# First operands of a gated feed-forward and of causal attention made in the stages in front, zeros in pieces, and sigmoid attention inside a ternary feed-forward

## The chip, the cores and the metric

The kernel runs on one core of a Trainium2 chip. The metric is the device time in microseconds (us) of one execution; less is better. Times of the kernel before are the median of three runs, and the profile is of one more execution.

## The reference

The state x has 2048 tokens of 256 numbers (32 sequences of 64). A second input of the same shape, the context c, is only read. Eight stages follow one another; each adds to x a function of its layer norm:

```
A  x += attention over the 256 columns of each 64-row block, c as keys and values, 8 heads
B  x += down(silu(gate(n)) * up(n)),          n = layernorm(x), 704 hidden
C  x += quantised attention of all 2048 tokens to all of c, 16 heads
D  h = layernorm(x);  h += causal attention(layernorm(h)*w + b) + bo, 16 heads of 128
   x += h + mixture of 4 experts on layernorm(h)
E  x += w_ct(relu(banded attention over the 256 columns of each block) * c)
F  x += ternary feed-forward: quantised rows and weights, 1024 hidden, silu(l0) * l1
G  x += sum over n of c * sigmoid(q^T c / sqrt(64)),  q = layernorm(x)
H  x += mixture of 8 experts (top 2) and a shared expert on layernorm(x)
```

In G each block of 64 rows of the state is its own matrix problem: scores are products of the block's q and c over its 64 rows, the sigmoid is taken of each score times 0.125, and the result is a product of c with these values. D begins with two norms in a row, as the attention norms once more what it is given.

## The kernel before

The state lies in SBUF for the whole run as 16 tiles `xs[i]` of 128 tokens by 256 (`x` in the trace), the context as `cs[i]`. Groups of four tiles (g = 0 to 3) share statistics and the transposed operand `xnT` or `hnT` (128 x 2 x 512). `ln_stats` (L74 to L88) takes a mean and a variance for each tile on DVE, adds epsilon on DVE (L85), and takes the power -1/2 on POOL (L87); `ln_apply` (L91) subtracts and scales on DVE; `transpose_to` (L97) makes two PE transposes, and ACT copies the result out of PSUM.

The stages run in the order of the letters, by the loop at the end of the program: before stage k runs, `weights(k + 1)` allocates the next stage's weights on the other side of SBUF (left and right in turn) and issues their loads on SP's queue. As sides alternate, the loads of stage k + 1 wait for the memory of stage k - 1. H's weights, 5.4 MB, are therefore loaded while G runs.

Outside F a scheduler orders the instructions of each engine from the program's dependences; every engine then works through its own list in order, and a waiting instruction holds those behind it. F is inside `tc.manual_schedule()`: its lists are in the order in which the program issues the instructions.

A (`run_A`) works in slots, step t of a loop of 16 x 8 + 53 steps, and finishes its tiles in order. B (`run_B`) norms a group, makes gate and up products in six chunks, `silu` on ACT (L486), the product on DVE, and four down products. Beside it runs a generator, `keys_and_values`, for stage C: keys, values and their maxima from the context tile by tile (`next(other)`); it begins with one memset of `vz` (L554), 128 x 16384 bf16, the values with zeros around them, and it is stepped once ahead of B's first norm.

C (`run_C`) is a loop over n, 16 tiles times 16 heads, and four steps more: scores on PE (L759), a move with a running maximum on DVE (L789), the exponential on ACT (L813), a cast on POOL (L823), a DMA transpose, and `product` (L772) four steps later. After the last head of a tile come `output`'s steps: a copy, the transposed reciprocal sums `rsT` (L730), two products, and the add to x on POOL (L752).

D begins (`run_D_attention`, `inputs`) with two norms of a group (`hs`, then `hn`), transposes and a scaled copy into `hnT` (L889), four value products (`vp`, L914, with the weights `Dwv`), and projections (L926) with rotations on DVE (`rtq`, L928), ACT and POOL. The bias `bo` is added to `hs` on POOL.

F treats a tile in steps with a lag each, so that step t holds parts of six tiles. For tile i: deviations and a power `s` on POOL; `xk`, two gained copies, their absolute maximum `am`, and the factors `sca` and `dqa` in `scales` (L1272 to L1277); rounding on ACT; transposes `xqT`; products `l` (L1314); `sl` by silu on ACT; `h` on DVE (L1329); squares on ACT; `rr` and `xr` on POOL (L1350, L1344); maximum and rounding `hq` on DVE (L1355, L1358); transposes `hqT`; the product `op`; the sum into x on DVE (L1380). The list of these parts with their lags is the manual order:

```python
for t in range(NT + 6):
    for part, lag in ((summed, 5), (first_transposes, 1), ..., (deviations, -1)):
        if 0 <= t - lag < NT:
            part(t - lag)
```

G (`run_G`) does for each tile: q on DVE, transposes of c and a DVE copy `cT`, eight score products, two sigmoids on ACT, eight products `gop`, and a sum into x on DVE (L1428). H (`run_H`) makes the constant `owner` on POOL (a memset and six selects, L1460 to L1464), norms a group, computes gate logits `hgp`, and runs 14 chunks of gate and up products (`pgate`, `pup`, L1523).

Of the kernel before, what the change touches and what calls it, by code (L numbers as in the profile page):

```python
# [31 lines left out]
def tile_net(ctx: ExitStack, tc: tile.TileContext, a: dict, out: bass.AP):  # L32
# [37 lines left out]


# [331 lines left out]
    def run_A(w, side):  # L403
        with ExitStack() as es:
# [6 lines left out]
            masks = []  # L411
# [18 lines left out]
            def start(t):  # L430
                if t in (16, 18):
                    next(parts)
                if t == 20:
                    for r in range(2):
                        masks.append(cp.tile([P, 1], F32, name=f"gmask{r}"))
                        V.tensor_tensor(masks[r], k["mask"][r], w["gamma"], ALU.mult)

# [16 lines left out]
    def load_B(wp):  # L454
# [8 lines left out]
        w["down_s"] = bcast_row(wp, a["L0_ffn_down_s"], D, "sdown")  # L463
        return w

    def run_B(w, side):
        with tc.tile_pool(name="Bw", bufs=2, side=side) as pool, tc.tile_pool(
# [3 lines left out]
            next(other, None)  # L471
            for g in range(NG):
                ids = range(4 * g, 4 * g + 4)
                xnT = norm_T(pool, psum, ids)
# [30 lines left out]
    def norm_T(pool, psum, ids, src=None, wb=None, keep=None):  # L505
# [3 lines left out]
        xnT = pool.tile([P, 2, 512], F32, name="xnT")  # L509
        for j, i in enumerate(ids):  # L510
# [5 lines left out]
            dst = xnT[:, :, j * P : (j + 1) * P]  # L516
            if wb is None:
                S.copy(dst, tp)
            else:
                for c in range(2):  # L520
                    S.activation(
                        dst[:, c, :], tp[:, c, :], AF.Identity, bias=wb[1][:, c : c + 1], scale=wb[0][:, c : c + 1]
# [21 lines left out]
    def keys_and_values(w):  # L544
# [9 lines left out]
        G.memset(vz, 0.0)  # L554
        w["spread"] = spread = qkp.tile([H, 4, 2, 64], F32, name="spread")
        with tc.tile_pool(name="C1v", bufs=1, side=side) as vp, tc.tile_pool(
# [5 lines left out]
            for i in range(NT):  # L562
# [30 lines left out]
                V.tensor_copy(kT[:, :, i * P : (i + 1) * P], tb)  # L593
                yield
# [49 lines left out]
    def run_C(w, side):  # L644
# [5 lines left out]
        with ExitStack() as es:  # L650
# [17 lines left out]
            with tc.tile_pool(name="C2w", bufs=1, side=side) as pool, tc.tile_pool(  # L668
# [113 lines left out]
                qs = out_ = iter(())  # L782
# [16 lines left out]
                for n in range(N + LAG):  # L799
# [34 lines left out]
                    if h in (0, 2, 3, 4, 5, 7, 8, 10, 11, 12):  # L834
                        next(qs, None)
                for _ in out_:
                    pass


    def load_D(wp):  # L840
# [22 lines left out]
    def run_D_attention(w, side, hs):  # L863
# [4 lines left out]
        with ExitStack() as es:  # L868
# [4 lines left out]
            hnT = [tpool.tile([P, 2, 512], F32, name=f"hnT{g}") for g in range(NG)]  # L873
# [3 lines left out]
            def inputs(g):  # L877
                ids = range(4 * g, 4 * g + 4)
# [767 lines left out]
```

## Time and profile before

| | |
|---|---|
| median of three runs | 2878.74 us (2876.58 to 2881.87) |
| profiled execution | 2879.53 us |
| its span, from first to last instruction | 2877.8 us |
| mean granted TensorE clock | 0.962 of full speed |

| stage | us from the span's start | PE busy | DVE | ACT | POOL | clock |
|---|---|---|---|---|---|---|
| A | 0 to 301.5 | 242.3 | 221.6 | 159.2 | 164.4 | 0.98 |
| B, keys of C | to 521.9 | 188.3 | 120.3 | 41.9 | 82.5 | 0.92 |
| C | to 1219.0 | 541.0 | 663.6 | 613.6 | 561.7 | 0.98 |
| D attention | to 1845 | 606.8 | 340.4 | 334.2 | 343.3 | 0.98 |
| D experts | to 2034 | 160.6 | 96.9 | 73.3 | 33.1 | 0.85 |
| E | to 2346.5 | 271.6 | 209.0 | 152.0 | 235.4 | 0.99 |
| F | to 2495.3 | 93.0 | 135.1 | 86.2 | 61.1 | 0.82 |
| G | to 2555.6 | 49.0 | 29.0 | 18.7 | 13.6 | 1.00 |
| H | to 2877.8 | 315.7 | 98.6 | 52.5 | 11.5 | 0.99 |

Busy times are us in the stretch. PE is TensorE's matmuls (PEld its weight loads), DVE VectorE, ACT ScalarE, POOL GpSimd, SP the engine that issues the DMAs. In a line of the timeline the first number is the start in us from the span's start, the second the time to the end of that instruction or, with xN, of N like it in a row; then engine, line of the program, operation, output, inputs and shapes; in brackets how long the engine had been idle and what released it. L numbers are lines of the kernel before.

### The profile page before, as it was taken

How to read it: one execution, taken by the hardware profiler on the slowest of the kernel's cores; microseconds unless marked ns; L12 is line 12 of the kernel's file. 1: busy time of each engine (PE TensorE's matmuls, PEld its weight loads, DVE VectorE, ACT ScalarE, POOL GpSimd, SP SyncE). 2: the span in 40 equal slices, each digit the busy share in tenths (PEclk: the TensorE clock that was granted, in tenths of full speed). 3: DMA queues.
4: the chain of work that ended last, by engine and by line, in shares of the span. 5: the costliest groups of instructions: out<-in, count | busy, mean ns of one | idle time of the engine just before them, and what ended most of it. 6: DMA issues, size and time to landing. Idle time of an engine off the chain costs nothing.

```text
span 2877.8 us, 44432 instructions
## 1 busy us (share of the span) xinstructions
PE 2468.2 (86%) x16072; PEld 1449.1 (50%) x16072; DVE 1914.5 (67%) x3989; ACT 1531.7 (53%) x2145; POOL 1506.4 (52%) x1681
## 2 busy tenths in 40 slices
PE   4989798777778777689999999789888976789999
PEld 2545344344444444346666666556555533445555
DVE  7877554699999999775455455663577669833332
ACT  1657221599999999655555555353345556521110
POOL 4655433588888888665555555311587754400000
PEclk9999899999999999889999999888999988999999
DMA  6553000499999999910000000001443300200000
GB/s 166 128 116 70 23 1 1 106 202 203 202 207 201 204 201 199 186 59 8 15 15 15 8 1 1 30 30 24 103 93 89 92 1 1 76 1 8 8 8 8
DMA packets 610599, 223.70 MB, mean 78 GB/s; under 512 B 547366, under 2 KB 600524, under 8 KB 605772
## 3 DMA queue, kind: packets, MB, share of 16 engines
q1 hardware_dynamic: 607308, 220.07, 35.0%
q8 instruction: 127, 2.08, 0.3%
q10 hardware_dynamic: 3072, 0.79, 0.2%
q14 instruction: 92, 0.75, 0.1%
HBM read 66.91 MB, written 18.87 MB: 30 GB/s over the span
## 4 chain that ended last, share of the span: by engine, by line
PE 50%; DVE 22%; issue 9%; POOL 5%; ACT 2%; DMA 1%; ACTq 0%; DVEq 0%; POOLq 0%; SPq 0%
DVE e L789 11%; PE yp L985 4%; PE ppq L926 3%; PE ppk L926 3%; PE hout L1502 3%; PE vp L914 3%; PE pgate L1523 3%; PE pup L1523 3%; PE sp L944 2%; PE ep L1072 2%; PE op L970 2%; PE hmp L1065 2%; PE sc L759 1%; PE op L495 1%; POOL e L286 1%
## 5 line engine op out<-in xcount | busy, mean ns | idle before, releaser
L813 ACT ACTIVATE ei<-e,nb,sq 128x2048 int16<-128x2048 f32 x256 | 535.4, 2092 | 43.4 <-DVE nb L810 39.7
L823 POOL CAST eb<-ei 128x2048 bf16<-128x2048 int16 x256 | 482.5, 1895 | 116.1 <-ACT ei L813 102.0
L759 PE MATMUL sc<-kT,qz 128*128 128x512 bf16 x1024 | 298.1, 382 | 142.0 <-DVE e L789 139.9
L246 DVE TENSOR_REDUCE negm<-s 128x2 f32<-128x512 f32 (+1 forms) x512 | 300.9, 611 | 130.6 <-PE s L242 127.4
L789 DVE TENSOR_SCALAR_CACHE_REDUCE e<-sc,mx 128x1024 f32<-128x1024 f32 x256 | 326.1, 1274 | 0.8 <-DVE nb L810 0.7
L789 DVE TENSOR_SCALAR_CACHE_REDUCE e<-sc 128x1024 f32<-128x1024 f32 x256 | 312.4, 1220 | 10.5 <-PE sc L759 10.5
L278 ACT ACTIVATE e<-s 128x1024 f32<-128x1024 f32 (+1 forms) x256 | 233.2, 915 | 152.8 <-PE s L274 117.3
L242 PE MATMUL s<-stk,stq 96*128 96x256 bf16 (+1 forms) x1024 | 192.2, 271 | 41.2 <-DMA d3k<-t3k 24.8
L759 PEld LDWEIGHTS <-qz 128*128 128x128 bf16 x1024 | 94.9, 97 | 261.2 <-issue 202.6
L934 POOL TENSOR_TENSOR rwq<-rwq,sin 128x512 f32<-128x512 f32 x64 | 81.1, 1268 | 240.1 <-ACT rwq L931 203.7
L274 PE MATMUL s<-stq,stk 128*128 128x256 bf16 (+1 forms) x1024 | 180.6, 262 | 10.8 <-DMA stq<-nm 5.4
L772 PEld LDWEIGHTS <-vz 128*64 128x64 bf16 x4096 | 123.2, 110 | 114.0 <-issue 113.9
L946 DVE TENSOR_REDUCE mx<-sp 128x4 f32<-128x512 f32 x64 | 44.3, 692 | 192.7 <-PE sp L944 192.7
L772 PE MATMUL av<-eT,vz 128*64 128x128 bf16 x4096 | 164.0, 223 | 7.3 <-DMA eT<-eb 7.2
L87 POOL TENSOR_TENSOR rstd<-ve,mhalf 128x1 f32<-128x1 f32 (+1 forms) x56 | 42.4, 757 | 240.9 <-DVE ve L85 145.9
L931 ACT ACTIVATE rwq<-ppq,dbq 64x512 f32<-64x512 f32 x128 | 87.4, 683 | 148.9 <-DVE rtq L928 148.0
L1533 DVE TENSOR_TENSOR hm<-pup,sl 128x512 f32<-128x512 f32 (+1 forms) x56 | 38.7, 692 | 191.1 <-PE pup L1523 187.4
L242 PEld LDWEIGHTS <-stq 96*128 96x128 bf16 x1024 | 93.6, 101 | 131.9 <-issue 108.6
L296 PE MATMUL o<-e,vmo 128*32 128x256 f32 (+1 forms) x2048 | 151.1, 367 | 7.4 <-POOL e L286 6.0
L1531 ACT ACTIVATE sl<-pgate 128x512 f32<-128x512 f32 (+1 forms) x56 | 33.4, 597 | 219.2 <-PE pgate L1523 219.1
L286 POOL TENSOR_SCALAR_AFFINE_SELECT e<-e 128x256 f32<-128x256 f32 (+1 forms) x256 | 133.2, 547 | 31.0 <-ACT e L278 30.3
L914 PE MATMUL vp<-Dwv,hnT 128*128 128x512 f32 x256 | 123.8, 605 | 4.0 <-ACT hnT L889 4.0
(349 smaller groups left out, 5518.5 us busy)
## 6 DMA issues: line engine op xcount, KB each, us to landing
stk<-d3k SPq DMA_DIRECT2D x96, 192.0 KB
stq<-d3q SPq DMA_DIRECT2D x96, 192.0 KB
d3k<-t3k SPq DMA_DIRECT2D x160, 64.0 KB
d3q<-t3q SPq DMA_DIRECT2D x96, 64.0 KB
eT<-eb SPq DMA_TRANSPOSE x256
fw<-in_L_ffn_w SPq DMA_DIRECT2D x3, 1024.0 KB
x<-in_x SPq DMA_DIRECT2D x16, 128.0 KB
c<-in_ctx SPq DMA_DIRECT2D x16, 128.0 KB
```

Of the source, the lines that this page charges most:

```text
L242: PE.matmul(sc[:, hh, lo:hi], qs[0:96, 2 * hp + hh, qc * P : (qc + 1) * P], ks[0:96, 2 * hp + hh, lo:hi], start=band is None, stop=True, s ...
L246: V.tensor_reduce(negm[:, qc, 2 * hp : 2 * hp + 2], sc[:, :, lo:hi], AX.X, ALU.max, negate=True)
L274: PE.matmul(sc[:, c, lo:hi], ks[:, h, lc * P : (lc + 1) * P], qs[:, h, lo:hi], start=True, stop=True)
L278: S.activation(e[:, :, lo:hi], sc[:, :, lo:hi], AF.Exp, scale=scale)
L759: PE.matmul(sc[:, k0 : k0 + 512], qz[i % 2][:, h, :], kT[:, h // 2, 1024 * part + k0 : 1024 * part + k0 + 512], start=True, stop=True,)
L772: PE.matmul(av[i][r0 : r0 + 64, h // 4, :], vz[:, kt, h // 4, h % 4, :], eT[:, kt, :], start=h == 0 and kt < 2, stop=h == H - 1 and kt >= ...
L789: V.tensor_scalar(e, scs.pop((n, part)), 1.0, mx[:, 0:1] if part else LOWEST, ALU.mult, ALU.max, accum_out=mx[:, part : part + 1],)
L813: S.activation(ei, es_.pop(n), AF.Exp, bias=nb, scale=sq[i][:, h : h + 1], accum_out=sums[i][:, h : h + 1],)
L823: G.tensor_copy(eb, eis.pop(n - 1))
L914: PE.matmul(vp, hnT[g][:, c, j * P : (j + 1) * P], wv[:, c, :], start=c == 0, stop=c == 1)
L926: PE.matmul(pp, wt[:, c, hh * P : (hh + 1) * P], hnT[g][:, c, :], start=c == 0, stop=c == 1)
L1523: PE.matmul(pp[:m], w[nm + "s"][:, c, cols], xnT[:, c, :], start=c == 0, stop=c == 1)
```

## The change

The dictionary `heads` hands work of a stage to the stage in front.

- B's first `xnT0` is made by `norm_parts` in A's last loop steps, from step 146, in A's pools. The keys of C start with B's first chunk instead of ahead of its norm.
- The memset of `vz` is split into one for each tile, issued as the keys are made.
- D's first `hnT0` is made by `inputs_D` in C's last loop steps (n of 256 and up), two of its steps each, in buffers of C. It computes the first norm into temporaries; D itself then computes the first norm again, into `hs`, and adds `bo`. The loads of the experts' weights are issued later in the program.
- G's parts are added to F's list, with lags 5 to 7 and a loop of NT + 8 steps; G itself returns at once. The sigmoid becomes 0.5 + 0.5 tanh(z/2): the half is taken by half row sums of c, from an ACT accumulation. Here q is made on POOL, `cT` copied on ACT, the result scaled on ACT (`gy`), and added to x on POOL. G's PSUM tiles share the tags of F's (`xqT`, `hqT0`, `hqT1`, `op`).
- In `scales` a tensor_scalar with the column `s` becomes a scalar_tensor_tensor with `s` broadcast.

```diff
@@ -68,6 +68,8 @@
+    heads = {}
@@ -408,7 +410,7 @@
             parts = attention_constants(cp, k)
-            masks = []
+            masks, head = [], []
@@ -435,6 +437,11 @@
+                if t == 146 and "B" in heads:
+                    head.append(heads.pop("B")(pool, psum))
+                if head:
+                    next(head[0], None)
@@ -461,6 +468,8 @@
         w["down_s"] = bcast_row(wp, a["L0_ffn_down_s"], D, "sdown")
+        w["xnT0"] = wp.tile([P, 2, 512], F32, name="xnT0")
+        heads["B"] = lambda pool, psum: norm_parts(w["xnT0"], pool, psum, "tp", range(4))
@@ -468,10 +477,14 @@
             other, stats = beside.pop() if beside else (iter(()), iter(()))
-            next(other, None)
+            if "B" in heads:
+                for _ in heads.pop("B")(pool, psum):
+                    pass
             for g in range(NG):
+                if g == 1:
+                    next(other, None)
                 ids = range(4 * g, 4 * g + 4)
-                xnT = norm_T(pool, psum, ids)
+                xnT = norm_T(pool, psum, ids, dst=None if g % 2 else w["xnT0"], bufs=1) if g else w["xnT0"]
@@ -502,24 +515,35 @@
-    def norm_T(pool, psum, ids, src=None, wb=None, keep=None):
+    def norm_parts(dst, pool, psum, tag, ids):
+        mv, rstd = ln_stats(pool, [xs[i] for i in ids], "hd")
+        yield
+        for j, i in enumerate(ids):
+            xn = pool.tile([P, D], F32, name="hdn", bufs=2)
+            ln_apply(xn, xs[i], mv, rstd, j)
+            yield
+            S.copy(dst[:, :, j * P : (j + 1) * P], transpose_to(psum, xn, tag, f"hdT_{i}"))
+        yield
+    def norm_T(pool, psum, ids, src=None, wb=None, keep=None, dst=None, bufs=2):
...
         mv, rstd = ln_stats(pool, [src[i] for i in ids])
-        xnT = pool.tile([P, 2, 512], F32, name="xnT")
+        xnT = pool.tile([P, 2, 512], F32, name="xnT", bufs=bufs) if dst is None else dst
...
@@ -551,7 +575,6 @@
         w["vz"] = vz = qkp.tile([P, NT, 4, 4, 64], BF, name="vz")
-        G.memset(vz, 0.0)
@@ -591,6 +614,7 @@
                 V.tensor_copy(kT[:, :, i * P : (i + 1) * P], tb)
+                G.memset(vz[:, i], 0.0)
@@ -779,7 +803,7 @@
                 scs, mxs, es_, eis, eTs = {}, {}, {}, {}, {}
-                qs = out_ = iter(())
+                qs = out_ = head = iter(())
@@ -833,6 +857,17 @@
                         next(qs, None)
+                    if n == N and "D" in heads:
+                        own = dict(stats=(small, H, "amq"), bn=(small, H, "rsq"), h=(pool, D, "xn"), hn=(pool, D, "qq"))
+                        def tile(nm):
+                            home, width, name = own[nm]
+                            return home.tile([P, width], F32, name=name)
+                        head = heads.pop("D")(tile, psum)
+                    if n >= N:
+                        next(head, None)
+                        next(head, None)
@@ -849,14 +884,63 @@
         w["gate"] = load(wp, [P, 2, 4], a["L1_ffn_w_gate"].rearrange("(c p) e -> p c e", p=P), "dgate")
+        w["hnT0"] = wp.tile([P, 2, 512], F32, name="hnT0")
+        heads["D"] = lambda tile, psum: inputs_D(w, None, w["hnT0"], 0, tile, psum)
...
+    def inputs_D(w, hs, hnT, g, tile, psum):
+        first = [None] * 4
+        for k in range(2):
+            t = tile("stats")
+            mv, ve, rstd = t[:, 0:8].rearrange("p (j c) -> p j c", c=2), t[:, 8:12], t[:, 12:16]
+            for j in range(4):
+                src = xs[4 * g + j]
+                if k == 1:
+                    src = first[j] if hs is not None else tile("h")
+                    if hs is None:
+                        V.tensor_scalar(src, xs[4 * g + j], *factors[j], ALU.subtract, ALU.mult)
+                b6 = tile("bn")[:, 0:6]
+                V.bn_stats(b6, src)
+                V.bn_aggr(mv[:, j, :], b6)
+                if j == 1:
+                    yield
+            V.tensor_scalar(ve, mv[:, :, 1], 1e-5, None, ALU.add)
+            G.tensor_tensor(rstd, ve, mhalf[:, 0:4], ALU.pow)
+            yield
+            if k == 0:
+                factors = [(mv[:, j, 0:1], rstd[:, j : j + 1]) for j in range(4)]
+                if hs is not None:
+                    for j in range(4):
+                        first[j] = hs[4 * g + j]
+                        V.tensor_scalar(first[j], xs[4 * g + j], *factors[j], ALU.subtract, ALU.mult)
+        for j in range(4):
+            if hs is None:
+                first[j] = tile("h")
+                V.tensor_scalar(first[j], xs[4 * g + j], *factors[j], ALU.subtract, ALU.mult)
+            hn = tile("hn")
+            V.tensor_scalar(hn, first[j], mv[:, j, 0:1], rstd[:, j : j + 1], ALU.subtract, ALU.mult)
+            if hs is not None:
+                G.tensor_tensor(first[j], first[j], w["bo"], ALU.add)
+            tp = transpose_to(psum, hn, "tp", f"hnTp_{4 * g + j}")
+            for c in range(2):
+                S.activation(
+                    hnT[:, c, j * P : (j + 1) * P], tp[:, c, :], AF.Identity,
+                    bias=w["ln1_b"][:, c : c + 1], scale=w["ln1_w"][:, c : c + 1],
+                )
+            yield
...
         with tc.tile_pool(name="Dh", bufs=1, side=side) as hpool:
-            w["we1"] = load(hpool, [P, 2, 4, D], a["L1_ffn_we1"].rearrange("(c p) e i -> p c e i", p=P), "we1")
-            w["be1"] = load(hpool, [P, 4, 2], a["L1_ffn_be1"].rearrange("p (e c) -> p e c", c=2), "be1")
-            w["be2"] = load(hpool, [4, D], a["L1_ffn_be2"].rearrange("o e d -> (o e) d"), "be2")
...
+            def experts():
+                w["we1"] = load(hpool, [P, 2, 4, D], a["L1_ffn_we1"].rearrange("(c p) e i -> p c e i", p=P), "we1")
+                w["be1"] = load(hpool, [P, 4, 2], a["L1_ffn_be1"].rearrange("p (e c) -> p e c", c=2), "be1")
+                w["be2"] = load(hpool, [4, D], a["L1_ffn_be2"].rearrange("o e d -> (o e) d"), "be2")
+            w["experts"] = experts
@@ -870,26 +954,16 @@
             psum = es.enter_context(tc.tile_pool(name="Dp", bufs=1, space=PSUM))
-            hnT = [tpool.tile([P, 2, 512], F32, name=f"hnT{g}") for g in range(NG)]
+            hnT = [w["hnT0"]] + [tpool.tile([P, 2, 512], F32, name=f"hnT{g}") for g in range(1, NG)]
...
             def inputs(g):
-                ids = range(4 * g, 4 * g + 4)
-                mv, rstd = ln_stats(pool, [xs[i] for i in ids])
-                for j, i in enumerate(ids):
-                    ln_apply(hs[i], xs[i], mv, rstd, j)
-                mv, rstd = ln_stats(pool, [hs[i] for i in ids])
-                for j, i in enumerate(ids):
-                    hn = pool.tile([P, D], F32, name="hn")
-                    ln_apply(hn, hs[i], mv, rstd, j)
-                    G.tensor_tensor(hs[i], hs[i], w["bo"], ALU.add)
-                    tp = transpose_to(psum, hn, "tp", f"hnTp_{i}")
-                    for c in range(2):
-                        S.activation(
-                            hnT[g][:, c, j * P : (j + 1) * P], tp[:, c, :], AF.Identity,
-                            bias=w["ln1_b"][:, c : c + 1], scale=w["ln1_w"][:, c : c + 1],
-                        )
+                for _ in inputs_D(w, hs, hnT[g], g, tile, psum):
+                    pass
+            def tile(nm):
+                return pool.tile([P, D if nm[0] == "h" else 16], F32, name=f"in_{nm}")
@@ -986,7 +1060,15 @@
             weights_of(0)
-            inputs(0)
+            if "D" in heads:
+                heads.pop("D")
+                inputs(0)
+            else:
+                mv, rstd = ln_stats(pool, [xs[j] for j in range(4)])
+                for j in range(4):
+                    ln_apply(hs[j], xs[j], mv, rstd, j)
+                    G.tensor_tensor(hs[j], hs[j], w["bo"], ALU.add)
+            w["experts"]()
@@ -1272,7 +1356,7 @@
                 V.reciprocal(sc, am)
-                V.tensor_scalar(sc, sc, s, 127.0, ALU.mult, ALU.mult)
+                V.scalar_tensor_tensor(sc, sc, 127.0, s.to_broadcast([P, n]), ALU.mult, ALU.mult)
@@ -1380,14 +1464,73 @@
+            def g_norm(i):
+                d = st[i]
+                mv, rstd = ln_stats(pool, [xs[i]], "g")
+                V.tensor_scalar(mv[:, :, 0], mv[:, :, 0], -1.0, None, ALU.mult)
+                d["q"] = pool.tile([P, D], F32, name="gq")
+                G.tensor_scalar(d["q"], xs[i], mv[:, 0, 0:1], rstd, ALU.add, ALU.mult)
+            def g_context(i):
+                d = st[i]
+                d["ctp"] = psum.tile([P, 2, 2, P], F32, tag="xqT", name="gcT")
+                for c in range(2):
+                    PE.transpose(d["ctp"][:, 0, c, :], cs[i][:, c * P : (c + 1) * P], ident)
+            def g_context_copy(i):
+                d = st[i]
+                d["cT"] = pool.tile([P, 2, P], F32, name="cT")
+                S.copy(d["cT"], d["ctp"][:, 0])
+                junk = tpool.tile([P, D], F32, name="gjunk")
+                d["half"] = pool.tile([P, 1], F32, name="half", bufs=3)
+                S.activation(junk, cs[i], AF.Identity, scale=0.5, accum_out=d["half"])
+            def g_scores(i):
+                d = st[i]
+                d["sp"] = []
+                for b in range(2):
+                    rows = slice(64 * b, 64 * b + 64)
+                    sp = psum.tile([P, 4, P], F32, tag=f"hqT{b}", name=f"gsp{b}").rearrange("p (n a) t -> p n (a t)", n=2)
+                    for n in range(2):
+                        PE.matmul(sp[:, n, :], d["q"][rows, n * P : (n + 1) * P], cs[i][rows, :], start=True, stop=True)
+                    d["sp"].append(sp)
+            def g_tanh(i):
+                d = st[i]
+                d["sg"] = []
+                for b in range(2):
+                    sg = pool.tile([P, 2, D], F32, name=f"gsg{b}")
+                    S.activation(sg, d["sp"][b], AF.Tanh, scale=0.0625)
+                    d["sg"].append(sg)
+            def g_product(i):
+                d = st[i]
+                d["gop"] = psum.tile([P, D], F32, tag="op", name="gop")
+                for b in range(2):
+                    rows = slice(64 * b, 64 * b + 64)
+                    for n in range(2):
+                        PE.matmul(
+                            d["gop"][rows, :], d["cT"][:, n, rows], d["sg"][b][:, n, :], start=n == 0, stop=n == 1
+                        )
+            def g_sum(i):
+                d = st[i]
+                y = pool.tile([P, D], F32, name="gy")
+                S.activation(y, d["gop"], AF.Identity, scale=0.5, bias=d["half"])
+                G.tensor_tensor(xs[i], xs[i], y, ALU.add)
+            parts = [
+                (summed, 5), (first_transposes, 1), (first_copy, 1), (second_transposes, 4), (second_copy, 4),
+                (hidden, 2), (g_product, 7), (g_sum, 7), (hidden_products, 1), (gates, 1), (second_norm, 3),
+                (squares, 2), (gained, 2), (g_context, 6), (g_context_copy, 6), (first_sizes, 0), (first_rounding, 0),
+                (second_rounding, 3), (g_scores, 6), (g_tanh, 6), (output, 4), (deviations, -1), (g_norm, 5),
+            ]
             deviations(0)
-            for t in range(NT + 6):
-                for part, lag in (
-                    (summed, 5), (first_transposes, 1), (first_copy, 1), (second_transposes, 4), (second_copy, 4),
-                    (hidden, 2), (hidden_products, 1), (gates, 1), (second_norm, 3), (squares, 2), (gained, 2),
-                    (first_sizes, 0), (first_rounding, 0), (second_rounding, 3), (output, 4), (deviations, -1),
-                ):
-                    if 0 <= t - lag < NT:
+            for t in range(NT + 8):
+                for part, lag in parts:
+                    if 0 <= t - lag < NT and (with_g or not part.__name__.startswith("g_")):
@@ -1395,6 +1538,8 @@
     def run_G(w, side):
+        if "FG" in STAGES:
+            return
```

More of the change, by code (lines that the diff above doesn't have):

```diff
@@ L515, in norm_T @@
             tp = transpose_to(psum, xn, "tp", f"xnT_{i}")
-            dst = xnT[:, :, j * P : (j + 1) * P]
+            part = xnT[:, :, j * P : (j + 1) * P]
             if wb is None:
-                S.copy(dst, tp)
+                S.copy(part, tp)
             else:
@@ L521, in norm_T @@
                     S.activation(
-                        dst[:, c, :], tp[:, c, :], AF.Identity, bias=wb[1][:, c : c + 1], scale=wb[0][:, c : c + 1]
+                        part[:, c, :], tp[:, c, :], AF.Identity, bias=wb[1][:, c : c + 1], scale=wb[0][:, c : c + 1]
                     )
@@ L1238, in run_F @@
     def run_F(w, side):
+        with_g = "FG" in STAGES
         if "ternary" in shared:
```

## Prediction

> **What bounds the kernel now.** One execution was profiled: 2879.53 us, a span of 2877.8 and 1.7 outside it. The busy shares of the whole span (PE 86%) say little, as eight stages with different limits follow one another. So I read the view by stretches first, at the seams that the change touches: stage B's start, ternary F, sigmoid G. After the stretch and its length come PE, PEld, DVE, ACT, POOL (busy us, instructions), granted clock, DMA share, GB/s.
>
> ```profile
> 301.00:311.00 10.00, 3.75 (x4) 1.17 (x4) 9.35 (x15) 1.31 (x3) 9.94 (x2) 0.50 0.38 90
> 321.00:331.00 10.00, 7.47 (x23) 2.94 (x21) 5.23 (x16) 2.20 (x7) 4.82 (x7) 0.65 0.00 0
> 331.00:521.00 190.00, 174.09 (x613) 89.34 (x612) 97.19 (x263) 38.44 (x81) 62.23 (x86) 0.98 0.00 1
> 2346.00:2495.00 149.00, 93.39 (x450) 52.76 (x448) 134.87 (x359) 86.22 (x145) 61.06 (x66) 0.82 0.00 1
> 2495.00:2556.00 61.00, 49.21 (x290) 27.89 (x290) 29.34 (x87) 18.67 (x33) 13.56 (x11) 1.00 0.31 90
> ```
>
> B's first 30 us leave PE nearly empty at half clock, and after that it is 92% busy: B is PE's, but for a late start. F is DVE's (134.87 of 149), with PE 63% and POOL 41% busy. G is PE's (49.21 of 61), with DVE half idle. Then the timeline at the seams.
>
> ```profile
> 301.59 13.75 POOL L554 MEMSET vz<- 128x16384 bf16 x1
> 304.02 11.34 DVE L85 TENSOR_SCALAR ve<-mv 128x4 f32<-128x4 f32 x1
> 332.48 0.70 PE L482 MATMUL gp<-xnT,wgate 128*128 128x512 f32 x1
> ```
>
> A 128x4 operation, 0.16 elsewhere, lasts 11.34: it ends as the memset ends. B's norm is behind it, so the first gate product comes 31 us after B begins.
>
> ```profile
> 1207.86 1.06 PE L772 MATMUL av<-eT,vz 128*64 128x128 bf16 x16 [0.95 <-DMA eT<-eb]
> 1217.65 0.35 SPq L107 DMA_DIRECT2D band<-in_c_band  x1
> 1219.03 0.43 DVE L82 BATCH_NORM_STATS2 bnst<-x 128x6 f32<-128x256 f32 x1 [9.59 <-POOL x L752]
> 1223.38 0.52 SPq L107 DMA_DIRECT2D Dwv<-in_L_ffn_wv  x1
> 1228.18 0.46 ACT L889 ACTIVATE hnT<-hnTp,ln_b,ln_w 128x128 f32<-128x128 f32 x1 [10.10 <-DMA Dwv<-in_L_ffn_wv]
> 1243.58 0.73 DVE L928 SCALAR_TENSOR_TENSOR rtq<-ppq,dbq,cos 128x512 f32<-128x512 f32 x1
> ```
>
> C ends with a serial tail, then D's loads on SP and D's norms on DVE run side by side.
>
> ```profile
> 2357.99 2.46 DVE L1284 SCALAR_TENSOR_TENSOR xk<-x,mv,fg 128x256 f32<-128x256 f32 x2
> 2419.29 2.49 POOL L1344 TENSOR_TENSOR xr<-h,fg 128x512 f32<-128x512 f32 x2
> 2420.82 0.99 DVE L1275 TENSOR_SCALAR sca<-sca,s 128x2 f32<-128x2 f32 x1
> 2495.44 1.27 POOL L1460 MEMSET owner<- 96x1408 bf16 x1 [5.78 <-DVE x L1380]
> 2555.21 0.42 DVE L1428 TENSOR_TENSOR x<-x,gop 128x256 f32<-128x256 f32 x1 [2.95 <-PE gop L1425]
> 2562.15 1.20 PE L1523 MATMUL pgate<-xnT,hwgate 128*128 128x512 f32 x1
> ```
>
> In F the 128x2 `sca` again ends with a POOL operation (2421.8). The last three are H's preparations, that start when F ends, G's last sum, and H's first product, 6.5 us after that sum.
>
> **1. A and B: the first xnT made in A's last steps; the memset in 16 pieces.** PE finishes A's own work near 298, and its gate products can then start at about 300 instead of 332.48. What stands in the way is small: 8 transposes on PE, 4 ACT copies of 0.37, 4 statistics of 0.42 and 4 applies of 0.40 on DVE, about 1.5 us where they displace A's last values. B's PE work stays: the 188 busy us in 301 to 521 hold some 14 of start-up, mostly at half clock, that shrink to about 8, so 182; at the 91.6% of the stretch 331 to 521 it lasts 198.6 us. From 301 that ends at 499.6 instead of 520.9: 21 us. Minus the 1.5 leaves 19.5. C's keys, which ran in B's first 30 us, now share B with it; they are covered by PE's own work, but PE, in order, can stall at the first kTp if POOL's chain is late. That is 3 to 6 us if uncovered. The memset pieces are 13.75/16 = 0.86 each; seven stand ahead of the first POOL work of the keys (6.0 us), which no one waits for at once. Bounds: -26 (no stall, better fill) to -12.
>
> **2. C and D: the first hnT made in C's last steps.** The reverse. DVE, POOL and PE are in order, and on PE the transposes hnTp of tiles 0 and 1 stand ahead of C's last product, tiles 2 and 3 ahead of rsT. They need a second norm: four applies and statistics of about 1.0 each on DVE from 1205.05 (after the last moved value), an add of 0.16, a POOL power behind the last cast, so the first hnTp at 1210.9; two transposes and two ACT writes of 0.81 through one bank bring the last product to 1214.3 (begun at 1207.86 before) and rsT to 1217.5 (1208.85). C ends 8.5 us later. Behind it wait: the `band` load at SP's head and, six loads later, `Dwv`, and x15's add on POOL, for which D's statistics wait. Since hnT was held by `Dwv` anyway (10.10 us of wait), having it early brings nothing itself. What is saved is D's second norm of the first group, 4.4 to 4.9 us of the chain on DVE and POOL that runs from 1219.03 to 1263.9 and releases rtq at 1243.58. Net: +8.5 - 4.7 = +3.8, say **+4**; -1 if the tiles go in without delaying the product, +9 if nothing is saved. The expert loads keep their place in SP's order; nothing.
>
> **3. `scales` by another instruction form.** `sca` lasts 0.99 against 0.23 where POOL is free, in 12 of 16 tiles: 9 us at most. The Trainium skill ("SBUF — State Buffer", Who interferes with whom) speaks against a gain: an exclusive port pair is taken by DVE's two-port forms, tensor_scalar among them, and also by a DVE operation with two SBUF inputs against a GpSimd one that reads SBUF. The new form reads `sc` and a broadcast `s`, two SBUF inputs, and `xr` reads SBUF. The trace agrees: the two-input `xk` above took 2.46 for two, where 0.47 is its shortest, under `xr`. By the first half of the rule alone the sum would be -9; by the whole of it, 0. I take 0.
>
> **4. F with G inside it, lags 5 to 7, sigmoid by tanh.** F's period is 8.84 us (L1380's ends from 2380.03 to 2477.33, 11 tiles, 97.3), with DVE full. Per tile G adds on DVE: statistics 0.42, aggregate 0.18, two small ones 0.30, of which 0.41 was there (G's own statistics already ran in F's gaps): DVE alone gives 9.3. POOL gets x's add (0.73), a power (0.55) and q (about 0.7 by the row of the add): 5.5 per tile, no bound; ACT reaches 8.0 (gy 0.47, cT 0.4, half sum 0.65, tanh 1.17), PE 7.9. But the queues are in order and there is a loop: hq of one step, hqT (1.06), gop of the older tile (1.57, from G's row), gy on ACT (0.47), x's add on POOL (0.73), the power (0.66), xr (2.5), amb's reduction and four small ones and hq (2.8), with hand-offs of about 0.1 to 0.2: 10.5. Part of it runs with the previous step, so I take **10.2** between 9.2 (DVE only) and 11.7 (loop plus held `sca`). Then F and G: 11 full steps from 2380, a drain of 2.3 periods (17.5 against 8.84 now is 2.0, plus two more lags), and for the last tile norm, q, scores, tanh, product, sum of 7.7. End = 2380 + 13.3 x 10.2 + 7.7 = 2523.4, against 2555.6: **-32**. The sigmoid's table load (1.28, once) goes too, within this.
>
> **5. What F and G covered.** H's weights (5.4 MB, 340 GB/s from 2495.5 to about 2513) and its constants start when F's memory comes free, and lay beside G. Now they start at G's end. On POOL the order is: owner memset 1.27, five selects of 1.40, and only then H's first power. That is 8.5 us, power 1.0, one apply 0.5, four transposes with copies at 0.9, gate logits 2.7: the first pgate comes 16.4 after G's last sum instead of 6.5. The weights, first needed then, land at +7.5 (gate) and +13 (up): covered. PE is idle for most of it, so its clock falls (0.50 in the first row above); 2 us more. **+12**, from +7 to +17.
>
> Sum: 2879.5 - 19.5 + 4 + 0 - 32 + 12 = 2844.0; the median stands 0.8 under the profiled execution: **2843** (1.2% faster).
>
> **The rivals.**
> *DVE sets F with G (period 9.2).* For it: DVE is 90% busy and POOL 41%. Against: `xr` is waited for already, and one more POOL operation stands ahead of it. End 2510: 2830. Also if the new form of `sca` isn't held.
> *The loop sets it, longer (11.7).* For: every hand-off crosses an engine, and a shared bank (gcT in xqT's, gsp in hqT's, gop in op's) gives PE one more wait each. End 2543.3: 2863.
> *B's start gains little.* The keys' kTp stalls PE as in the stretch 471 to 481, where PE did 5.4 of 10: then -10 instead of -19.5, 2853.
> *Slower.* The loop in F with G: it becomes serial, each tile passing through POOL twice with PE waiting in its queue. The other parts together are -3.5, so F with G decides when its end is later than 2559: a period of (2559 - 2387.7)/13.3 = 12.9, which is 46% over today's. At 13.5 it is 2887. Against it: no single engine has more than 9.3.
> *The change does nothing in C and D* is within the bounds of 2.
>
> **How the numbers follow.** Forecast 50%, short period 20%, long period 14%, B's start 9%, slower 5%, even 2%. A measurement of this kernel tells 0.2%, some 6 us, from no change: faster 0.93, same 0.02, slower 0.05. The range reaches to the short period with part 1's better end, and to the long one: 2818 to 2864.
>
> **What would show it.** Right: first gp at 300 to 303; last av of C near 1214 and band near 1226; L1464's sums every 10.2 in F with G; owner's memset directly after G's last add, and pgate 16 after it; `sca` still near 1 in most tiles. Wrong: a period of 9 or 12, PE waiting for kTp in B, Dwv no later than now, or pgate waiting for hwgate.

## The result, and the profile after

The changed kernel takes 2842.23 us (median of four runs, 2840.02 to 2843.49) against 2879.16 for the kernel before (now four runs): a ratio of 0.9871, with a 95% interval of 0.9854 to 0.9888. The prediction was 2843. The profiled execution of it took 2840.02 us, its span is 2838.3 (before: 2879.53 and 2877.8).

A sum that comes out right may be right by two errors, so I cut the traces at the same instruction in each kernel. All times in the table are from an instruction's start or end in one profile to another's in the same profile.

| stretch | before | after | change | predicted |
|---|---|---|---|---|
| start to A's last add | 301.5 | 298.4 | -3.1 | |
| A's last add to C's first score | 229.3 | 212.3 | -17.0 | -19.5 with the row above |
| C's first score to its last cast | 673.1 | 674.7 | +1.5 | 0 |
| C's last cast to D's first rtq | 39.6 | 44.0 | +4.4 | +4 |
| D's first rtq to F's first xk (D and E) | 1104.3 | 1106.2 | +1.9 | 0 |
| F's first xk to G's last product | 207.3 | 167.5 | -39.8 | -32 |
| G's last product to H's first pgate | 7.0 | 19.5 | +12.6 | +12 |
| pgate to the end of H's last sum | 312.6 | 312.2 | -0.4 | 0 |

A's part scatters by itself: in the profiles of the twelve kernels of the experiments, whose A is the same or nearly so, its last add ends between 294.5 and 298.9, and that of tile 5, long before any edit, between 165.2 and 170.5 over all fourteen. The experiments were also run later than the changed kernel, together with the kernel before, which then took 2874.55 to 2877.39 us (medians of seven runs) instead of 2879.16. So the totals of two kernels of this study say little under some 5 us; those of all twelve lie 2 to 8 us under what their stretches give, and the experiments are read by stretch.

The view by stretches of the kernel after, with the columns as before (length, then PE, PEld, DVE, ACT, POOL, clock, DMA share, GB/s): B's start, B, F with G, H's start.

```profile
294.00:304.00 10.00, 9.49 (x26) 4.04 (x25) 7.26 (x29) 4.34 (x7) 7.99 (x11) 1.00 0.58 158
304.00:334.00 30.00, 24.22 (x74) 10.33 (x73) 17.02 (x44) 6.19 (x14) 20.12 (x27) 0.89 0.00 1
334.00:500.00 166.00, 149.53 (x538) 78.65 (x537) 83.59 (x227) 31.02 (x67) 56.61 (x78) 0.98 0.00 1
2336.00:2494.00 158.00, 116.79 (x692) 66.01 (x692) 141.45 (x391) 112.58 (x228) 85.21 (x107) 0.90 0.00 1
2504.00:2523.00 19.00, 6.44 (x25) 4.85 (x26) 10.59 (x37) 2.77 (x5) 13.05 (x11) 0.57 0.97 285
```

PE is busy from B's first microsecond, at full clock in the first row (in the 30 us behind it 81% and 0.89). F with G is DVE's, 90% busy, with PE at 74% instead of 63. H's start is now bare: PE does 6.4 us of work in 19, at a clock of 0.57, while the weights come in. The timeline at the seams, B, D, F and H in turn:

```profile
294.94 1.98 PE L495 MATMUL gp<-xnT,wgate 128*128 128x512 f32 x4 [0.51 <-ACT rd L311]
298.47 6.35 POOL L617 MEMSET vz<- 128x1024 bf16 x7
301.68 0.45 DVE L87 TENSOR_SCALAR ve<-mv 128x4 f32<-128x4 f32 x1
...
1195.06 1.06 PE L796 MATMUL av<-eT,vz 128*64 128x128 bf16 x16
1207.86 0.36 SPq L109 DMA_DIRECT2D band<-in_c_band  x1
1213.58 0.52 SPq L109 DMA_DIRECT2D Dwv<-in_L_ffn_wv  x1
1218.15 9.57 PE L988 MATMUL vp<-Dwv,hnT 128*128 128x512 f32 x16 [9.22 <-DMA Dwv<-in_L_ffn_wv]
...
2399.73 2.50 POOL L1428 TENSOR_TENSOR xr<-h,fg 128x512 f32<-128x512 f32 x2
2399.96 1.06 DVE L1359 SCALAR_TENSOR_TENSOR sca<-sca,s 128x2 f32<-128x2 f32 x1
...
2504.72 1.27 POOL L1605 MEMSET owner<- 96x1408 bf16 x1
2513.13 2.00 POOL L89 TENSOR_TENSOR rstd<-ve,mhalf 128x4 f32<-128x4 f32 x2
2522.74 3.76 PE L1668 MATMUL pgate<-xnT,hwgate 128*128 128x512 f32 x4
```

The first gate product even precedes A's last add (by 3.5 us). `ve`, that the memset held for 11.34 us, takes 0.45. From `band` to the first `vp` D still waits for `Dwv`, 9.22 us on PE. `sca` in its new form takes 1.06; the old one took 0.99. And `owner` is made ahead of H's first power.

### The profile page after: what moved, and what is told of

Read it like the earlier page. It is cut to its first block, busy times and chain, and to the rows that moved or that the text cites. A ratio compares the mean times of both kernels' runs of the same rounds, so it can differ in the third digit from the quotient of the medians.

```text
span 2838.3 us, 44529 instructions
## 1 busy us (share of the span) xinstructions
PE 2448.6 (86%) x16072; PEld 1439.3 (51%) x16072; DVE 1901.2 (67%) x3986; ACT 1544.1 (54%) x2208; POOL 1533.8 (54%) x1741
## 3 DMA queue, kind: packets, MB, share of 16 engines
q1 hardware_dynamic: 607308, 220.07, 35.5%
## 4 chain that ended last, share of the span: by engine, by line
PE 48%; DVE 22%; issue 9%; POOL 7%; ACT 2%; DMA 1%; SPq 0%; ACTq 0%; DVEq 0%; POOLq 0%
DVE e L813 11%; PE yp L1059 4%; PE ppq L1000 4%; PE ppk L1000 3%; PE hout L1647 3%; PE vp L988 3%; PE pgate L1668 3%; PE pup L1668 3%; PE sp L1018 2%; PE ep L1154 2%; PE op L1044 2%; POOL e L288 2%; PE hmp L1147 2%; PE sc L783 1%; PE op L508 1%
## 5 line engine op out<-in xcount | busy, mean ns | idle before, releaser
L1678 DVE TENSOR_TENSOR hm<-pup,sl 128x512 f32<-128x512 f32 (+1 forms) x56 | 38.7, 691 | 190.6 <-PE pup L1668 186.9
L89 POOL TENSOR_TENSOR rstd<-ve,mhalf 128x1 f32<-128x1 f32 (+1 forms) x44 | 29.9, 680 | 178.7 <-DVE ve L87 86.2
```

## The experiments

Twelve kernels, each an edit of the changed kernel.

**1. The first norm back in B (e1), and the memset in one piece again (e2).**

```diff
-                if t == 146 and "B" in heads:
+                if t == 1460 and "B" in heads:
```
```diff
+        G.memset(vz, 0.0)
...
-                G.memset(vz[:, i], 0.0)
```

> Against the changed kernel (2842.2): B's first norm is put back into B, the memset stays in pieces and the keys still start with the first chunk. If the early norm itself is what moved B's start, B waits again for statistics, power, applies and four transposes, about 7 to 8 us after A's last add, and the first gate product comes near 306 instead of 294.9: 2850 to 2853. If most of the old 31 us came from the memset ahead of the norm, that is all that is lost; if the two are worth the same, the whole 20 us of part 1 come back: 2862.

> Against the changed kernel: the memset of vz is one piece again (13.75 us), the early norm stays. If the memset matters only because B's norm stood behind it, nothing is lost: 2842 within 3. If it still holds a 128x4 operation on DVE for its whole length, B's products hT stand behind that on DVE, PE's banks fill, and 8 to 10 us come back: 2850 to 2852.

Measured: 2847.06 and 2846.12 us. From A's last add to C's first score they take 223.1 and 219.7 instead of 212.3: the early norm is worth 10.7 us, the pieces 7.4, together 18.1, about the 17.0 that the changed kernel gained in this stretch. That C's keys start with B's first chunk, as they do in all three kernels, wasn't tried alone. The first gate product of e1 comes at 306.7, 11.3 after A's last add (7 to 8 expected). In e2 it comes as early before that add as in the changed kernel, and then:

```profile
297.06 13.75 POOL L578 MEMSET vz<- 128x16384 bf16 x1
300.26 10.57 DVE L87 TENSOR_SCALAR ve<-mv 128x4 f32<-128x4 f32 x1
```
```profile
304.00:314.00 10.00, 0.57 (x3) 0.60 (x4) 9.96 (x17) 0.00 (x0) 6.81 (x1) 0.66 0.00 0
```

The first fence is its timeline, the second its stretch from 304 to 314. A `ve` of a later norm is held until the memset ends at 310.8, the `vall` of C's keys and B's products `hT` stand behind it on DVE, and PE does 0.57 us of work in 10: it waits 9.8 us, to the end of `vall`. The memset stalls B even if B's own first norm is long done.

**2. Without the early hnT (e3), and with its transposes later (e7).** In e3 D makes its own; in e7 the first norm's statistics and half of the second's stay in C's last steps, and the rest comes behind C's output.

```diff
-                    if n == N and "D" in heads:
+                    if n == N + 100 and "D" in heads:
```
```diff
                     if n >= N:
-                        next(head, None)
-                        next(head, None)
+                        next(head, None) if n < N + 3 else None
                 for _ in out_:
                     pass
+                for _ in head:
+                    pass
```

> Against the changed kernel: D makes its first hnT itself, as before. By part 2 of the prediction C's last product and rsT are no longer delayed (8.5 us) and D's start takes its second norm back (4.7): 2838.4, faster by 3.8; C's last product ends near 1189 instead of 1196.1. If the early hnT is a gain, as the change has it, it is slower by 4 to 9: 2846 to 2851.

> Against the changed kernel: the early hnT stays in C's tail, but its transposes stand on PE behind C's last product, rsT and op. By part 2 the delay of C's end goes (8.5 us from the last cast to the last product, as in the run without the early hnT) and the second norm stays saved: from the last cast to rtq 36 us, against 44.0 in the changed kernel and 39.6 in before: 2834. If the delay comes from DVE or POOL rather than PE's order, the last product still ends 10 us after the last cast: 2842.

Measured: 2830.26 and 2831.33 us. C's last product ends 4.95 and 4.89 us after its last cast, as before the change (4.94), against 10.69 with the early hnT in its place: PE's order was the delay. From the last cast to rtq e3 takes 39.6, 4.5 us less than the changed kernel (3.8 expected); the rest of its lead in the profiles lies in A, B and C (3.2) and behind rtq (2.2), where the other kernels differ as much. But e7 takes 40.2, not 36: its delay is gone, and the early operand still brings nothing. Its timeline says why:

```profile
1192.74 0.35 SPq L109 DMA_DIRECT2D band<-in_c_band  x1
1195.10 0.41 DVE L924 TENSOR_SCALAR qq<-xn,amq 128x256 f32<-128x256 f32 x1 [9.28 <-POOL amq L911]
1201.17 0.75 DVE L84 BATCH_NORM_STATS2 bnst<-x 128x6 f32<-128x256 f32 x2 [1.23 <-PE hnTp L99]
1201.22 0.38 SPq L109 DMA_DIRECT2D Dwv<-in_L_ffn_wv  x1
1215.44 1.88 PE L1001 MATMUL ppq<-hnT,Dwq 128*128 128x512 f32 x4
1219.38 0.72 DVE L1003 SCALAR_TENSOR_TENSOR rtq<-ppq,dbq,cos 128x512 f32<-128x512 f32 x1
```

`rtq` doesn't wait for `ppq`, which ends at 1217.32; it follows DVE's other work without a pause. DVE reaches D's own statistics only at 1201.17, 8.4 us behind `band` (1.4 in the changed kernel), since the early applies, each waiting for the transposes of the one before, now stand between C's end and D: what D is spared is done just ahead of it. `Dwv` is issued 8.5 us behind `band` instead of 5.7, after the last of these transposes; why it waits for them wasn't tried, and it isn't what `rtq` waited for.

**3. G after F again (e4).**

```diff
-        with_g = "FG" in STAGES
+        with_g = False
...
-        if "FG" in STAGES:
-            return
```

> Against the changed kernel: G runs after F again, with its sigmoid; everything else stays. F's period goes from 9.35 to 8.8 and G takes its 60 us, H's constants and weights lie beside G: F's start to pgate takes 214.3 as before instead of 187.1, so 27 us come back: 2869. If H's late start has another cause than the lost cover, pgate stays 16 us behind G's last sum and it is 2879.

Measured: 2862.89. F's first xk to pgate takes 214.1 us (before 214.3; changed 187.1): the 27 us are these two parts and nothing else (the total, 2869 expected, is lower by the other stretches). pgate follows G's last product after 8.0.

**4. The old form in scales, and DVE's order.** In e8 the line of `scales` is the old one. In e5 the operations stay and DVE's order changes: the new entries split `first_sizes`, `second_rounding`, `deviations` and `g_norm` behind their reductions.

```diff
-                (first_sizes, 0), (first_rounding, 0),
-                (second_rounding, 3), (g_scores, 6), (g_tanh, 6), (output, 4), (deviations, -1), (g_norm, 5),
+                (first_sizes, 0), (second_size, 3),
+                (deviation_stats, -1), (g_stats, 5), (first_scales, 0), (first_rounding, 0),
+                (second_rounding, 3), (g_scores, 6), (g_tanh, 6), (output, 4), (deviation_power, -1), (g_norm, 5),
```

> Against the changed kernel: scales has its tensor_scalar back, all else stays. By part 3 both forms are held by xr alike: sca near 1.0 in most tiles, and 2842 within 3. If the new form is what freed DVE, it is 8 to 11 us slower: 2850 to 2853.

> Against the changed kernel: DVE's order in F with G. The reduction of xr (of the step before) and the two pairs of statistics, that read one tile each, are put between the maximum am and the factor sca, so that they run while POOL makes xr, and the small operations on two SBUF inputs come after it. If DVE's own list, with sca's 0.83 us of being held, sets the period, as the trace of the changed kernel has it (DVE busy 94%, nothing waited for), sca takes about 0.2 and the period falls from 9.35 to about 8.5: 11 us less, 2831. If the loop through PE, ACT and POOL of the prediction is what binds, the period stays, and sca, 2.4 us later in the step, makes the rounding and PE later: 2842 to 2850.

e8 measured 2837.13 us; F with G takes 168.3 against 167.5, and the group of `sca` between 2370 and 2480 (busy, mean ns, idle) is, in the changed kernel and in e8:

```profile
L1359 DVE SCALAR_TENSOR_TENSOR sca<-sca,s 128x2 f32<-128x2 f32 x11 | 11.5, 1043 | 0.4
```
```profile
L1359 DVE TENSOR_SCALAR sca<-sca,s 128x2 f32<-128x2 f32 x11 | 11.6, 1053 | 0.4
```

The two forms are held alike, as the Trainium skill ("SBUF — State Buffer", Who interferes with whom) has it for a two-port form and for two SBUF inputs. e5 measured 2827.94; its F with G takes 159.5, 8.0 less, at a median period of 8.62 instead of 9.35. DVE's list was the bound. But the holding, which was expected to go, only moved: what came next was held instead. Lines of the changed kernel, then of e5:

```profile
2408.05 0.69 DVE L1370 TENSOR_REDUCE am<-xk 128x2 f32<-128x512 f32 x1
2408.84 0.23 DVE L1356 TENSOR_SCALAR am<-am,s 128x2 f32<-128x2 f32 x1
```
```profile
2406.19 0.69 DVE L1377 TENSOR_REDUCE am<-xk 128x2 f32<-128x512 f32 x1
2406.80 1.21 DVE L1449 TENSOR_REDUCE amb<-xr 128x1 f32<-128x1024 f32 x1
2407.54 2.50 POOL L1438 TENSOR_TENSOR xr<-h,fg 128x512 f32<-128x512 f32 x2
2409.00 1.07 DVE L1363 TENSOR_SCALAR am<-am,s 128x2 f32<-128x2 f32 x1
2410.31 0.16 DVE L1366 SCALAR_TENSOR_TENSOR sca<-sca,s 128x2 f32<-128x2 f32 x1
```

`sca` is at 0.16, and a tensor_scalar on 128x2, 0.23 in the changed kernel, waits for the end of `xr` at 2410.04 (in some steps both are held). The two changes cancel. The 0.7 us that the step lost are mostly pauses: an operation that needs the result of a reduction starts 0.1 us after its end, one that doesn't starts 0.08 before it. From the start of `am`'s reduction to the next operation it is 0.61 instead of 0.79, for `amb`'s 1.13 instead of 1.32, for each of the two aggregates 0.10 instead of 0.22. In the first two full steps of e5, when POOL has no sums of G yet, nothing is held, and the period is 7.75.

**5. H's start.** Three kernels: `owner` issued after the first group's norm (e6); H on the side of SBUF that nobody uses while F with G runs, its loads issued at F (e9); the same with H's working buffers on F's side (e12, the second diff besides the first).

```diff
-        return ("left", "right")[STAGES.index(stage) % 2]
+        return "left" if stage == "H" else ("left", "right")[STAGES.index(stage) % 2]
...
+            if STAGES[k] == "F":
+                ahead[k + 2] = weights(k + 2)
```
```diff
-            pool = es.enter_context(tc.tile_pool(name="Hw", bufs=2, side=side))
+            pool = es.enter_context(tc.tile_pool(name="Hw", bufs=2, side="right"))
```

> Against the changed kernel: the constant owner (a memset and six selects on POOL) is issued after the first group's norm in H instead of ahead of it. By part 5 of the prediction POOL's 8.4 us stand between G's last sum and the first power; without them the first pgate comes about 10 us after G's last sum instead of 18, unless it then waits for hwgate, expected at 7.5: 2834 to 2836. If the weights set it anyway, at most 2 us are won: 2840.

> Against the changed kernel: H's weights and constants get the other side of SBUF, which nobody uses while F with G runs, and are loaded and made during F. If H's late start is the loss of the cover that G gave (part 5 of the prediction, +12.6 as measured from G's last sum to pgate), it comes back: pgate about 7 us after G's last product, as before, or sooner: 2828 to 2832. If the first group's norm, that waits for the last tiles or for memory, is what takes the time, owner's absence only saves POOL's part, about 3 us as in the run with owner later: 2839.

> As the run on the free side, against the changed kernel, but H's working buffers lie on F's side again, so that its statistics can't be put into F's lists; weights, owner and share stay on the free side. In that run F's period was 10.6 to 12.2 instead of 9.35, with DVE waiting at H's statistics of a tile for G's sum of that tile. If these statistics in DVE's queue are the cause, the period is 9.35 again, G's last product is 52 us ahead of before's, and pgate follows it after 13 to 16 us (norm and transposes are no longer hidden, owner and the weights are): 2835 to 2838. If the loads or POOL's constants beside F slow it, the period stays above 10: 2848 or more.

e6 measured 2834.32: pgate 16.8 after G's last product instead of 19.5. The scheduler still put the memset and two selects ahead of the first power, which comes 4.2 us after G's last sum instead of 8.5; and the first two applies of the norm, under the other selects, take 2.82 us instead of 0.74. So only part of the 8.4 us went. e9 measured 2845.67, no gain: pgate comes 7.5 after G's last product, as expected of the lost cover, but F with G takes 185.5 instead of 167.5. With the memory free, H's statistics were put into DVE's list in F:

```profile
2397.37 0.43 DVE L84 BATCH_NORM_STATS2 bnst<-x 128x6 f32<-128x256 f32 x1 [1.30 <-POOL x L1522]
```

They need G's sum of the tile, which is late in the step, and DVE, the bound, stands still for it (9.0 us in nine steps) besides the time that they take themselves. In e12 they stay out: 2834.28, a period of 9.34 again in most steps (one of 10.57), F with G 171.5, pgate 13.5 after G's last product. So the loads and the constants beside F cost no more than 4 us; the rest of the 18 is H's early norm, the statistics and what follows them.

**6. Together.** e10 is without the early hnT and has a further order in F: on DVE the gained copies and `sca` ahead of `h`, on PE `l` last in a step. e11 has H on the free side besides.

```diff
+                (g_product, 7), (g_sum, 7), (first_sizes, 0), (first_scales, 0), (g_context, 6), (g_context_copy, 6),
+                (g_scores, 6), (g_tanh, 6), (output, 4), (hidden, 2), (first_rounding, 0), (second_norm, 3), (squares, 2),
+                (gained, 2), (second_size, 3), (deviation_stats, -1), (g_stats, 5), (second_rounding, 3),
+                (deviation_power, -1), (g_norm, 5), (hidden_products, 1), (gates, 1),
```

> Two parts together: without the early hnT (worth 6.9 us from C's last cast to D's end), and F with G in a new order: on DVE the gained copies, their maximum and the factor sca come ahead of h, so that no operation with two SBUF inputs or a small tensor_scalar stands under xr; PE makes l last in a step. DVE's list without the holding is about 7.8 us, PE 7.3 and ACT 7.3: if DVE's list sets the period, 8.0 and 2817 (7 and 18 less). If hand-offs between the engines bind at the 8.6 of the first reordering, 2825.

> The two parts of the run before and H's weights and constants on the free side. If the three are independent the gains add: about 12 below the run before, 2805 to 2808. If H's loads or its early norm disturb F, the period of F is longer than in the run before and some of it is lost: 2812 or more.

e10: 2821.07, F with G 156.5, most periods at 8.36 to 8.42: better than 8.62, not the 8.0 of DVE's list. Again something else is held:

```profile
2396.85 0.57 DVE L1366 SCALAR_TENSOR_TENSOR scb<-scb,rr 128x1 f32<-128x1 f32 x1
```

`scb` has two SBUF inputs, stands under `xr`, and takes 0.57 or more in most steps (0.16 elsewhere); without it a step of 8.36 has 7.95. In the steps near 9, `sca` or `dqa` is held besides, under x's add on POOL (`dqa` 0.72 instead of 0.15). PE waits for hq in most steps (15.8 us in nine), so it isn't the bound. e11: 2813.86 (2811.01 to 2818.59; 2805 to 2808 expected, had the gains just added), pgate 7.6 after G's last product, F with G 160.7, 4.2 more than in e10. H's statistics are in F's list here too, but in this order DVE waits only 0.4 us for G's sum before one of them. e11 beats both kernels: 0.9788 of the kernel before, 0.9763 to 0.9814, where the changed kernel has 0.9854 to 0.9888.

## Why the prediction was right

That the median came within 1 us is luck in part. Between the profiled executions 35.5 us were forecast and 39.5 measured, as F with G gained 7.8 more and the other stretches gave half of it back; and the profiled run of the changed kernel is the fastest of its four, 2.2 under their median. Direction, places and order of size of the parts were forecast; one mechanism, in part 4, was not the one at work.

**Part 1** said -19.5 and the two rows of the table give -20.1, of which 3.1 are A's scatter. Its split wasn't given. The pieces were costed as work for which no one waits; e2 shows that the single memset, with the early norm in place, costs 7.4 us of B, by the same holding that the trace of before showed for the norm. The first gate product came at 294.9, not at 300 to 303. What is short of 19.5 may be the keys: from 300 to 520 PE waited 11.4 us for kTp on POOL's chain, before the change 8.4.

**Part 2** is right in both terms: from the last cast to `band` 22.4 us against 13.7, +8.7 (said: 8.5), and from `band` to rtq 21.6 against 25.9, -4.3 (said: -4.7). e3 gets both back. What the prediction saw as one of its bounds, -1 if the tiles go in without delaying the product, is e7: +0.7, since there the second norm is moved, not spared. One of its readings is off: before the change hnT was held by the norm, not by `Dwv`:

```profile
1227.41 0.69 PE L97 MATMUL hnTp<-ident,hn 128*128 128x128 f32 x2 [8.69 <-DVE hn L91]
```

hnT at 1228.18 follows these transposes at once. But the first `vp` came 11.9 us behind `band`, and with hnT ready it comes 10.3 behind it, waiting for `Dwv` (ten loads behind `band`, not six): the early operand brings PE 1.6 us there and no more.

**Part 3** is right: by e8 the form makes 0.8 us of F with G, no more than e2 differs there with the form and order of the changed kernel (168.6 against 167.5).

**Part 4** had the right direction and place, and a size off: -32 said, -39.8 measured. The step that failed is the loop (hq, hqT, gop, x's add, rr, xr, amb, hq). There is none within a step: amb has lag 3 and xr lag 2, so amb reduces the `xr` of the step before, the loop goes round once in two steps, and nothing on DVE waits for POOL's `xr` of this one (0.6 us of waits on DVE between 2370 and 2480). The period of 10.2 was 9.35, DVE's list: some 7.75 of work, 0.7 of the pauses that e5 shows, and 0.9 of `sca` being held. That is the first rival, which the prediction gave 20% where it gave the loop 50%; over 13.3 periods it makes -11.3. The end took 4.8 us more than the formula's 2.3 periods and 7.7: F's last four sums came after 24.3 us instead of 21.5, and G's last sum 10.05 after F's. From -32.2 this makes -38.7; to G's last sum, where the formula ends, -38.8 was measured. What bounds these last steps wasn't tried. (The times that the prediction gives for the ends of L1380's sums are their starts; the period is the same.)

**Part 5** is right at +12.6 and in its order: POOL's constants, then the power, then PE at half clock. e4, e9 and e12 show that the lost cover is the cause: pgate comes 6.5 us after G's last sum in the kernel before, 18.1 in the changed one (18.4 said), 12.0 in e12 with weights and constants ahead, 6.0 in e9 with the norm ahead as well. e6 shows that POOL's order is a part of it. The half clock cost 1.8 us (2 said): four pairs of transposes at 0.69 instead of 0.44, and the gate logits 3.58 instead of 2.82. The weights were there in time, as said: pgate followed the gate logits without a wait.

Of the other rivals, B's start gained 17.0 and not 10 (PE waited 2.9 us for kTp on POOL's chain up to 340), and the slower one stayed far off: 9.35 against a period of 12.9.

The rest of the 39.5 us between the profiled executions is +3 in stretches that the change doesn't touch or hardly; one profile of each can't tell it from scatter. The end of the range, 2818, is 5 us lower than the two terms named for it make it (2830 - 6.5).

## What to carry to other kernels

When a stage is merged into the one in front, list what lay hidden beside it (loads, constants, the next stage's first norm) and find them another cover; here 12.6 of 39.8 us went back that way. If a scheduler fills the gaps, giving it memory also gives it leave to put a late operand's reader into the list of the engine that bounds. And of an operand made early ask what else its consumer waits for, and which instructions in order stand behind the making of it: the early xnT was worth 10.7 us, the early hnT cost 4.4. On an engine whose list is the bound, put something independent behind each reduction (0.7 us of a step of 9.35 here).

## What was not expected of the hardware

- Which DVE operation is held under a POOL operation that reads SBUF was a matter of order among those that can be: with `sca` moved (e5) a tensor_scalar of 128x2 took 1.07 instead of 0.23, with that moved too (e10) a scalar_tensor_tensor of 128x1 took 0.57 instead of 0.16. A reduction, statistics and, in e10, a tensor_scalar of 128x1 in the same place kept their times (amb 1.21, statistics 0.42, amb's factor 0.18).
- A hold lasted to the end of one POOL operation, also when the next followed at once: `sca` at 2399.96 took 1.06, while the two products of `xr`, 1.27 each, ran from 2399.73 to 2402.23.
- A memset of 13.75 us, that only writes, held a 128x4 tensor_scalar for 11.34 us before and for 10.57 in e2; pieces of 0.9 held it for 0.3.
